# The order of the first transfers in a four-stage network: rows, weights, rows, tables, zeros

## The chip, the core and the metric

The kernel runs on one core of a Trainium2 chip. The core has five engines with queues of their own: PE (TensorE, matrix products), DVE (VectorE), ACT (ScalarE), POOL (GpSimd) and SP (SyncE), which here only starts transfers between the DRAM and the on-chip memory. The transfers are carried out by 16 DMA engines. PEld stands for TensorE's loads of weights, and a q after an engine's name for its sequencer.

The metric is the device time of one execution in microseconds (us), the median of several. L130 means line 130 of the kernel.

## What is computed

The input is X, 8 sequences of 512 rows of 256 values in float32. Four blocks follow, each with a normalised input, a normalised output and a residual sum:

```python
x = L0_attn_X
x = x + _layernorm(_L0_attn_ref(_layernorm(x), Wq, Wk, Wv, Wo, lq1, lk1, lq2, lk2, rms_scale))
x = x + _layernorm(_L0_ffn_ref(_layernorm(x), wqkv, q_scale, k_scale, wo, ln_g, ln_b, w1, b1, w2, b2))
x = x + _layernorm(_L1_attn_ref(_layernorm(x), Wqk_t, Wv_t, Wo_t, tau_t, ...))
x = x + _layernorm(_L1_ffn_ref(_layernorm(x), gate_w, w1, b1, ln1_g, ln1_b, w2, b2, ln_g, ln_b))
```

The first block is a causal attention with 16 heads in which two softmaxes are subtracted:

```python
Q, K, V = (proj(Wq), proj(Wk), proj(Wv))
lam = exp(sum(lq1 * lk1)) - exp(sum(lq2 * lk2)) + LAMBDA_INIT
attn = softmax(A1) - lam * softmax(A2)          # A1, A2: causal scores of the two halves
O = attn @ V
O = O / sqrt(mean(O * O) + EPS) * rms_scale * (1.0 - LAMBDA_INIT)
return Oc @ Wo.T
```

The second is a local attention of two layers (windows of 128 rows, 8 heads) with a gated feed-forward part; its queries and keys are normalised, scaled by q_scale and k_scale and rotated by a table of sines and cosines. The third is an attention by distances between rows. The fourth sends each row to 2 of 8 experts, by a table of rows in DRAM.

## The kernel before

**Stages.** The function network (L1230) calls four stages one after the other, each over all 8 sequences: diff (first block), local, diffusion and experts. A sequence is 4 tiles of 128 rows. All of X stays on chip in one tile, self.x, from which xb(b) takes the 4 row tiles of sequence b.

**What is loaded first.** begin (L119) loads the constants (L123), sets a small tile of -0.5 on GpSimd and loads the eight sequences of X, 512 KB each (L130). Then network calls, in this order:

- load_diff (L206): the first stage's weights wv, wq, wk and wo, 512 KB each, in one loop (L214); the scale rms in four small pieces (L218); VectorE multiplies wo by it (L220); the vectors lq and lk of both softmaxes (L225, L226), their products and sums (L227, L229) on VectorE, their exponentials (L230) on ScalarE, and from these the factor nlam (L234 to L239).
- clear_rows (L981): a 512 KB tile of zeros, set by GpSimd (L985), is stored 136 times (L988) into four tables of rows in DRAM, xrows and yrows for each of two parts. The tables are used by the stage of the experts only.
- load_projections (L453) for layer 0 of the local stage: the weight qkv, 1536 KB (L457), the rotary table rot, 512 KB (L459), and for q_scale and k_scale each three small pieces of a tile s (L462, L464). GpSimd multiplies the four parts of rot by s (L467). These tiles are in a pool named early. The local stage calls the function again for layer 1 (L531).
- diff (L258): the first stage itself.

**The first stage.** For a sequence, rows(b) normalises X (L155 and L157 on VectorE, L146 and L147 on GpSimd, L161 on VectorE, into h). prepare(b) turns h by transposes on TensorE (L172), copies the result to hT (L139 on ScalarE, L141 on VectorE), and makes v with wv (L180, L289). queries and keys make qT (L299) and kT (L310) with wq and wk for four heads at a time. A loop then runs over slots, eight to a step, eight steps to a sequence. In a slot, TensorE makes scores (sc, L322, and turned, sa, L332), VectorE adds the mask and takes maxima (L335, L336), ScalarE takes exponentials (e, L339), and GpSimd clears what lies above the diagonal (L342). Each step also has products with v (po, L355), sums of e by GpSimd (L360), and a division (pn, L373; L375 and L376 on ScalarE). The line of all matmuls that go through the helper mm is L180.

**What sets the order.** The text gives the operations and their dependencies. A planner fills each engine's queue before the kernel runs, from a model of the costs: an operation that stands early in the text can go to a later place in its engine's queue if the planner expects its input late. In the run, each queue is worked off in that fixed order, and semaphores hold an instruction until its inputs are there. All transfers of the opening are started by SyncE; its queue waits, too, when an earlier transfer has to be complete before another one starts.

Of the kernel before, what the change touches and what calls it, by code (L numbers as in the profile page):

```python
# [17 lines left out]
NB = 8  # L18
NT = 4
# [93 lines left out]
class Net:  # L113
# [5 lines left out]
    def begin(self, ctx):  # L119
        nc = self.nc  # L120
        keep = ctx.enter_context(self.tc.tile_pool(name="keep", bufs=1))
        self.const = keep.tile([P, C_N], F32, name="const", tag="const")
        nc.sync.dma_start(self.const, self.a["const"])  # L123
        self.ident = self.const[:, C_ID:C_ID + P]
        self.mhalf = keep.tile([P, 64], F32, name="mhalf", tag="mhalf")
        nc.gpsimd.memset(self.mhalf, -0.5)
        self.x = keep.tile([P, NB * NT, D], F32, name="x", tag="x")
        xin = self.a["L0_attn_X"].rearrange("b (t p) d -> p b t d", p=P)
        for b in range(NB):
            nc.sync.dma_start(self.x[:, b * NT:(b + 1) * NT, :], xin[:, b])  # L130

    def xb(self, b):
        return self.x[:, b * NT:(b + 1) * NT, :]
# [359 lines left out]
    def local(self, nb, early, first):  # L493
# [3 lines left out]
        with ExitStack() as ctx:  # L497
# [204 lines left out]
            for b in range(min(2, nb)):  # L702
                begin(b)
# [4 lines left out]
            for c in range(total + 1):  # L708
                if c + 1 < total:
                    r.add(rotated(c + 1))  # L710
                for u, calls in enumerate(slots):
                    if c < total:
                        scores(c, u)
                    if u == 2 and c:
                        g.add(gated(c - 1))
                    half = (len(calls) + 1) // 2
                    for f in calls[:half]:
                        f()
                    before = (c, u - 1) if u else (c - 1, 7)
                    if before in weights:  # L720
                        turned(*before)
                    for f in calls[half:]:
                        f()
                    if before[1] % 2 and (before[0], before[1] // 2) in sums:
                        attend(before[0], before[1] // 2)
                    if u in (2, 6) and c + 2 < nb:
                        save(c + 2) if u == 2 else begin(c + 2)
                qkv.pop(c - 1, None)
# [500 lines left out]
@with_exitstack  # L1229
def network(ctx: ExitStack, tc: tile.TileContext, a, out, nb=NB, parts=(1, 2, 3, 4)):  # L1230
    net = Net(tc, a, out)
    net.begin(ctx)
    if 4 in parts:
        net.scratch(ctx)
    with ExitStack() as local:
        early = local.enter_context(tc.tile_pool(name="early", bufs=1))
        with ExitStack() as w:
            if 1 in parts:
                net.load_diff(w)
            if 4 in parts:  # L1240
                net.clear_rows(w)
            if 2 in parts:
                first = net.load_projections(early, 0)
            if 1 in parts:
                net.diff(nb)
        if 2 in parts:
            net.local(nb, early, first)
    with ExitStack() as w:
        if 3 in parts:
            net.load_diffusion(w)  # L1250
            net.diffusion(nb)
    with ExitStack() as w:
        if 4 in parts:
            net.load_experts(w)
            net.experts(nb)
    if 4 not in parts:
        for b in range(nb):
            tc.nc.sync.dma_start(out.rearrange("b (t p) d -> p b t d", p=P)[:, b], net.xb(b))
# [39 lines left out]
```

## Time and profile before

| what | value |
|---|---|
| median of 3 runs | 4472.37 us (4471.97 to 4474.58) |
| the profiled execution | 4470.47 us |
| its span, first to last instruction | 4468.7 us |
| mean granted TensorE clock | 0.919 |
| bytes read from and written to HBM | 54.59 MB and 98.57 MB |
| stores of zeros (L988) | 136 of 512 KB, issued from 24.04 to 197.9 us |
| first and last mask of the first stage (L342) | 53.9 and 1167.1 us |
| first transposes of the local stage (L520) | 1196.9 us |
| first scatter of rows to the experts (L1094) | 3838.0 us |

How to read the lines that follow: the page gives each engine's busy time, its share of the span and its count of instructions; then the span in 40 equal slices of 112 us, where a digit is the busy share of a slice in tenths. A line of the table of waits has the waiting engine, line and operands, whom it waited for, and then the total, the number of times and the longest. A line of a timeline has the start, the duration, the engine, the line of code, the operation, output and inputs with their shapes, the count of merged instructions and, in brackets, how long the engine was idle before and what ended it. The lines of SPq are the transfers as SyncE starts them: their duration there is that of the start, not of the transfer.

### The profile page before, as it was taken

Reading aid. Unit: us, or ns where it says so; the run is one execution under the profiler, and the core shown is the slowest. Engines: PE = TensorE matmul, PEld = TensorE weight load, DVE = VectorE, ACT = ScalarE, POOL = GpSimd, SP = SyncE. Lnnn points to the kernel's source line nnn. Section 1 sums busy time; section 2 is a strip of 40 time slices with the busy share of each in tenths; the row PEclk is TensorE's granted clock in tenths of the full one; section 3 lists DMA queues with packets and bytes.
Section 4 is the critical chain, followed back from the end, with each engine's and each line's share of the span. In section 5 each row is a group of like instructions: output and inputs, shape, how many; then the busy total and the mean of one; then the engine's idle time right before and its main releaser. Section 6 shows DMA issues by size and latency. Waiting matters only on the chain.

```text
span 4468.7 us, 56341 instructions
## 1 busy us (share of the span) xinstructions
PE 3856.2 (86%) x21108; PEld 2000.8 (45%) x21108; DVE 2553.4 (57%) x4680; ACT 1760.7 (39%) x3300; POOL 1944.6 (44%) x1689
## 2 busy tenths in 40 slices
PE   8899999999778889999999998779999999488780
PEld 3333444433355555555555555433443434455450
DVE  6677777666365555444455554255666664454755
ACT  3455555555243333343433333224444443033230
POOL 3566666666565444444444454120111110441626
PEclk9999999999799999999999999889999999599895
DMA  9800000000000000000000000000000000421211
GB/s 382 347 6 1 6 6 6 6 6 6 30 3 3 3 3 3 3 22 9 27 8 8 8 8 10 13 19 1 1 1 1 1 1 1 156 76 59 79 55 61
DMA packets 101710, 160.97 MB, mean 36 GB/s; under 512 B 24956, under 2 KB 72384, under 8 KB 101440
## 3 DMA queue, kind: packets, MB, share of 16 engines
q1 hardware_dynamic: 95296, 140.59, 8.9%
q0 software_dynamic: 6144, 16.79, 1.2%
q8 instruction: 169, 2.77, 0.2%
q14 instruction: 101, 0.83, 0.1%
HBM read 54.59 MB, written 98.57 MB: 34 GB/s over the span
## 4 chain that ended last, share of the span: by engine, by line
PE 63%; POOL 16%; DVE 8%; SPq 4%; issue 4%; ACT 3%; DMA 1%; another core or an unknown queue 0%; POOLq 0%; DVEq 0%; ACTq 0%
PE lpa L180 8%; PE lpp L180 5%; PE tsc L832 5%; PE sc L322 5%; SPq L988 4%; PE pp L180 4%; PE po L355 3%; POOL ss L555 3%; PE py L180 3%; PE lqk L180 2%; PE tpo L855 2%; PE sa L332 2%; POOL qk L563 2%; PE ph L180 2%; PE lsc L597 2%
## 5 line engine op out<-in xcount | busy, mean ns | idle before, releaser
L339 ACT ACTIVATE e<-sa 128x1024 f32<-128x1024 f32 (+3 forms) x512 | 359.5, 702 | 355.1 <-PE sa L332 352.7
L360 POOL TENSOR_TENSOR e<-e,e 128x1536 f32<-128x1536 f32 (+2 forms) x192 | 451.6, 2352 | 93.6 <-PE po L355 83.7
L332 PE MATMUL sa<-qT,kT 32*128 32x512 f32 (+3 forms) x2048 | 432.6, 499 | 9.5 <-ACT e L339 9.1
L336 DVE TENSOR_REDUCE spread<-sc 128x2 f32<-128x256 f32 (+3 forms) x512 | 422.5, 825 | 15.6
L322 PE MATMUL sc<-kT,qT 32*128 32x128 f32 (+3 forms) x2048 | 422.7, 495 | 6.3 <-ACT kT L310 3.1
L844 DVE TENSOR_REDUCE spread<-tsc 128x2 f32<-128x1024 f32 x256 | 311.5, 1221 | 191.7 <-PE tsa L841 162.7
L847 ACT ACTIVATE te<-tsa 128x1024 f32<-128x1024 f32 x256 | 261.6, 1024 | 379.7 <-PE tsa L841 379.1
L180 PE MATMUL lpa<-ghT,lw 128*128 128x512 f32 (+1 forms) x768 | 378.2, 651 | 13.9 <-ACT ghT L525 13.9
L611 ACT ACTIVATE lp<-lp,lnm 128x256 f32<-128x256 f32 (+1 forms) x512 | 239.8, 470 | 217.5 <-DVE lnm L603 121.5
L335 DVE TENSOR_TENSOR sc<-sc,const 128x256 f32<-128x256 f32 x512 | 218.9, 428 | 181.5 <-PE sa L332 156.0
L146 POOL TENSOR_SCALAR rs<-mv 128x1 f32<-128x1 f32 (+1 forms) x208 | 41.5, 199 | 625.3 <-DVE mv L157 607.7
L841 PE MATMUL tsa<-tqT,tkT 32*128 32x512 f32 x1024 | 293.1, 652 | 22.9 <-DVE spread L844 22.7
L832 PE MATMUL tsc<-tkT,tqT 32*128 32x512 f32 x1024 | 302.5, 643 | 1.2 <-DVE tkT L818 0.7
L322 PEld LDWEIGHTS sc<-kT,qT 32*128 32x128 f32 x2048 | 159.9, 189 | 281.7 <-issue 123.0
L619 POOL TENSOR_TENSOR lp<-lp,lrs 128x256 f32<-128x256 f32 (+1 forms) x128 | 103.2, 828 | 395.7 <-DVE lrs L612 395.7
L615 POOL TENSOR_TENSOR lp<-lp,lrs 128x1024 f32<-128x1024 f32 x64 | 121.6, 1900 | 312.2 <-DVE lrs L612 302.3
L180 PEld LDWEIGHTS lpa<-ghT,lw 128*128 128x128 f32 (+1 forms) x768 | 147.1, 197 | 229.6 <-issue 197.6
L180 PE MATMUL lqk<-qkv,lhT 128*128 128x512 f32 x512 | 240.8, 613 | 1.4 <-ACT lhT L139 0.8
L342 POOL TENSOR_SCALAR_AFFINE_SELECT e<-e 128x512 f32<-128x512 f32 x256 | 160.5, 640 | 186.2 <-ACT e L339 186.1
L1168 ACT ACTIVATE ehT<-eht,enorm 128x128 f32<-128x128 f32 x320 | 120.2, 457 | 289.6 <-PE eht L1164 255.6
L555 POOL TENSOR_TENSOR ss<-ss,mhalf 128x16 f32<-128x16 f32 x64 | 186.2, 2909 | 82.5 <-DVE ss L554 81.7
L355 PE MATMUL po<-e,v 128*32 128x512 f32 (+3 forms) x2048 | 190.1, 454 | 19.4 <-POOL e L342 19.0
(256 smaller groups left out, 7743.7 us busy)
## 6 DMA issues: line engine op xcount, KB each, us to landing
xrows<-zero SPq DMA_DIRECT2D x68, 512.0 KB
yrows<-zero SPq DMA_DIRECT2D x68, 512.0 KB
ex<-xrows SPq DMA_DIRECT2D x80, 128.0 KB
yrows<-ey SPq DMA_DIRECT2D x80, 128.0 KB
ew<-in_L_ffn_w_dram SPq DMA_DIRECT2D x16, 512.0 KB
x<-in_L_attn_X_dram SPq DMA_DIRECT2D x8, 512.0 KB
saved<-x SPq DMA_DIRECT2D x8, 512.0 KB
lx<-saved SPq DMA_DIRECT2D x8, 512.0 KB
```

The lines of the kernel that those rows point to most:

```text
L180: self.nc.tensor.matmul(out, lhsT=l, rhs=r, start=i == 0, stop=i == len(pairs) - 1)
L322: nc.tensor.matmul(sc[:, i, :w], lhsT=qT[g, self.tok(t)], rhs=kT[g, :w], start=True, stop=True)
L332: nc.tensor.matmul(sa[:, i, :S - k * P], lhsT=kT[g, self.tok(k)], rhs=qT[g, k * P:], start=True, stop=True)
L336: nc.vector.tensor_reduce(self.spread[n % 2][:, t, g0:g0 + 2, 0 if n % 2 else 16], sc[:, :, :w], AX.X, ALU.max, negate=True)
L339: nc.scalar.activation(x[:, h0:h0 + 2, :], sa[:, :, :S - k * P], AF.Exp, scale=0.25)
L355: nc.tensor.matmul(pos[n][group(g), k * P:], lhsT=seqs[b][1][:, k, 4 * r + g, :], rhs=x[:, g, :], start=k == 0, stop=k == 2)
L360: nc.gpsimd.tensor_add(y, y, es.pop((n, k)))
L555: nc.gpsimd.tensor_tensor(sf, sf, self.mhalf[:, :2 * FH], ALU.pow)
L832: nc.tensor.matmul(sc[:, i, :], lhsT=qT[q, self.tok(t)], rhs=kT[q, :], start=True, stop=True)
L841: nc.tensor.matmul(sa[:, i, :], lhsT=kT[q, self.tok(k)], rhs=qT[q, :], start=True, stop=True)
L844: nc.vector.tensor_reduce(self.spread[n % 2][:, t, g0:g0 + 2, 16], sc, AX.X, ALU.max, negate=True)
L847: nc.scalar.activation(es[n, k][:, h0:h0 + 2, :], sa, AF.Exp)
```

## The change

The loop over the eight transfers of X becomes a function of its own. begin calls it for sequence 0 only. network calls it for sequences 1 to 7 after load_diff, then load_projections, and only then clear_rows.

```diff
@@ begin
         self.x = keep.tile([P, NB * NT, D], F32, name="x", tag="x")
+        self.load_rows(range(1))
+
+    def load_rows(self, seqs):
         xin = self.a["L0_attn_X"].rearrange("b (t p) d -> p b t d", p=P)
-        for b in range(NB):
-            nc.sync.dma_start(self.x[:, b * NT:(b + 1) * NT, :], xin[:, b])
+        for b in seqs:
+            self.nc.sync.dma_start(self.xb(b), xin[:, b])
@@ network
             if 1 in parts:
                 net.load_diff(w)
+            net.load_rows(range(1, NB))
+            if 2 in parts:
+                first = net.load_projections(early, 0)
             if 4 in parts:
                 net.clear_rows(w)
-            if 2 in parts:
-                first = net.load_projections(early, 0)
             if 1 in parts:
                 net.diff(nb)
```

In the order of the text, SyncE's transfers are then: const, x of sequence 0, wv, wq, wk, wo, rms, lq and lk, x of sequences 1 to 7, qkv, rot, s, and the 136 stores of zeros. No transfer, no operation and no byte is added or left out.

## The prediction

> **What bounds the kernel now.** I read the page first (busy shares and the 40 slices), then the table of waits of the first 300 us, then the timelines of SyncE, GpSimd, ScalarE and TensorE around the two places that the change touches. The page gives TensorE as the engine that sets the pace, and one odd stretch at the start: the DMA engines are full for the first two slices and idle after.
>
> ```profile
> PE 3856.2 (86%) x21108; PEld 2000.8 (45%) x21108; DVE 2553.4 (57%) x4680; ACT 1760.7 (39%) x3300; POOL 1944.6 (44%) x1689
> ...
> PE   8899999999778889999999998779999999488780
> ...
> DMA  9800000000000000000000000000000000421211
> ```
>
> The reader is to see that TensorE is at 8 tenths exactly in the slices in which the DMA engines are full (slices are 112 us). The table of waits for 188 to 232 us (engine and line, whom it waited for, total us, times, longest) says who lost time there:
>
> ```profile
> ACT e L339 <- PE sa L332: 24.3, 9, 18.2
> POOL rot L467 <- DMA s<-in_L_ffn_q_scale_dram: 22.0, 1, 22.0
> DVE sc L335 <- PE sa L332: 21.3, 5, 16.9
> PEld po L355 <- POOL e L342: 18.3, 3, 15.2
> PE po L355 <- POOL e L342: 15.4, 2, 14.3
> ```
>
> So it is a chain: GpSimd waits for a transfer, TensorE for GpSimd, ScalarE and VectorE for TensorE. The timeline of GpSimd shows where it stands (start, duration, line, operation, count, idle before):
>
> ```profile
> 187.12 0.63 POOL L342 TENSOR_SCALAR_AFFINE_SELECT e<-e 128x512 f32<-128x512 f32 x1
> 209.78 1.41 POOL L467 TENSOR_TENSOR rot<-rot,s 128x256 f32<-128x256 f32 x2 [22.03 <-DMA s<-in_L_ffn_q_scale_dram]
> 211.14 0.64 POOL L342 TENSOR_SCALAR_AFFINE_SELECT e<-e 128x512 f32<-128x512 f32 x1
> 211.75 1.41 POOL L467 TENSOR_TENSOR rot<-rot,s 128x256 f32<-128x256 f32 x2
> ```
>
> The multiplication of the rotary table, which only the local stage needs (its first matmuls come at 1197 us), stands in GpSimd's queue among the masks of the first stage, and nothing behind it can run. SyncE's timeline says why its operand is late: 136 stores of zeros are ahead of it.
>
> ```profile
> 24.04 41.73 SPq L988 DMA_DIRECT2D xrows<-zero  x34
> ...
> 154.18 43.72 SPq L988 DMA_DIRECT2D yrows<-zero  x34
> 197.94 2.09 SPq L457 DMA_DIRECT2D qkv<-in_L_ffn_wqkv_dram  x1
> 200.07 1.12 SPq L459 DMA_DIRECT2D rot<-in_rotary_dram  x1
> 201.24 1.00 SPq L462 DMA_DIRECT2D s<-in_L_ffn_q_scale_dram  x1
> ```
>
> The second place is the start. TensorE's timeline has its first projection waiting for the first weight, which SyncE issued behind all eight x transfers:
>
> ```profile
> 10.73 2.19 PE L172 MATMUL pt<-const,h 128*128 128x128 f32 x8 [10.73 <-DVE h L161]
> 18.80 1.19 PE L180 MATMUL pv<-wv,hT 128*128 128x512 f32 x1 [5.87 <-DMA wv<-in_wvT_dram]
> ```
>
> **What the Trainium skill says.** "TensorE: Matmul & The Clock Gate", section "Architectural detail: the array is 16× 32×32, not 1× 128×128": GpSimd's queue is a strict FIFO; the trace agrees (one waiting multiplication held masks whose inputs were made at about 189 to 198 us until 211.14). "DMA: Bandwidth & Descriptors", section "Queues, rings and completion order": on each DMA engine descriptors are consumed in the order of the ring, so a small transfer queues behind all bytes issued before it; the trace agrees (the 32 KB of s were in use only at 209.78, behind 136 stores). The first page's section "Part 1: The HAM clock gate (the "warmup" mystery)" has the array at half clock until it has been busy for some 3.4 us; here the first pv weight loads are 0.86 us apart until 24.05 and 0.43 after, so about six matmuls were slow, near 2.6 us in all.
>
> **The change, part by part.** The sum is made against the profiled execution: span 4468.7, device time 4470.5, so 1.8 us lie around the span; the median of the runs shown is 4472.4, 1.9 above that execution.
>
> Bytes and instructions are the same; only SyncE's order changes. Does that queue follow the text? In the trace it does at the start: const, eight x, wv, wq, wk, wo, rms, lq, lk, zeros, qkv, rot, s. GpSimd's doesn't: L467 stands far behind the first norm, which is later in the text; a planner set it by its own estimate of when s lands, and that was 22.0 us short.
>
> (1) *rot and s ahead of the zeros.* Ahead of s will be const 771.5 KB, x 8 x 512, weights 4 x 512, lq and lk 4 x 128, qkv 1536 and rot 512: 9475 KB or 9.70 MB. In before 301 GB/s x 25.0 us = 7.5 MB had moved at 25 us (windows view, first stretch); the other 2.2 MB at the 406 GB/s of the next stretches take 5.4, so 30.4. The six s transfers take 3.9 us to issue (201.24 to 205.16) and the last was in use 4.6 us later: s is there at about 39 us at worst. GpSimd has nothing to do from 19.5 (end of the last L147) to 53.93 (first mask): wherever the planner puts the four multiplications (0.73 us each, 2.9 in all) in that gap, their wait is covered by 14 us of slack; were they put behind the first masks, they would cost up to 2.9 and no wait.
>
> What the stall costs is read from the pace, not from the 22.0, since TensorE still had work. Line L375 (a reciprocal on ScalarE) runs once per step, eight steps to a sequence. Every eighth start, from ScalarE's timeline: 177.77, 331.93, 468.68, 604.84, 741.45, 878.06, 1014.12. The distances are 154.2, then 136.8, 136.2, 136.6, 136.6, 136.1. The stretch with the stall is 154.2 - 136.5 = 17.7 us longer than the others. This includes the slow clock after it (0.82 for 211.9 to 232). What is next late without it? In the same steps of other sequences nothing stands in for it: these distances are alike to 0.7 us, and TensorE is busy for 97.0 of 100 us at 300 to 400. So 17.7; the lower end 14.8 if the multiplications return to the path.
>
> (2) *First weights ahead of seven x transfers.* 512 KB at 406 GB/s is 1.29 us; seven are 9.0. wv, in use at 18.8, is then there at about 9.8; wq and wk follow at 1.29 each. The next late thing is hT: its second half is copied by VectorE at 12.96 for 0.69, so pv starts at 13.65: 5.15 earlier. Below this it is not certain: VectorE is in order too, and wo's scaling (L220, which waited for rms until 24.41; 9.0 earlier is 15.4) and the lq products (24.41 to 27.66 with waits, 3.3 us) may be planned ahead of that copy. Then hT would be at 15.4 + 3.3 + 0.7 = 19.4, 0.6 later than pv now: a loss of 0.6. Above it: without the pause from 12.92 to 18.80 the array may be warm sooner, up to 2.6 more, 7.8 in all. I take 4.5, since the copy of hT has the higher claim on being early (its inputs exist at 12.9, before rms can land), less a little for the mix. After pv the path is pv, pq, pk, kT, first scores at 33.12; all of it moves along.
>
> (3) *Seven x transfers later.* x1 follows lq and lk at about 15, x7 at about 15 + 6 x 1.29 + latency, 24 to 25. Needed early: nothing. TensorE turns the second sequence at 220.89; VectorE makes all 32 statistics before 22.0 only because it was idle. Moved, they fill VectorE's gaps; from 33.1 to 50.0 it was busy 11.65 of 16.9. If planned before x lands, a statistic holds VectorE by the planner's error, which was 22.0 in 210 us, so about 2 to 3 us at 25, before the first scores at 28.6. Cost 0, upper end 3.
>
> (4) *Zeros later.* They start about 2.1 MB of qkv and rot (5 us) and the issues of s later and end near 205 to 210, as the last transfer did. Their first user (L1094, the scatter of rows) runs at 3838 us. The next thing in SyncE's queue, L510 at 317.45, waited for GpSimd's x (103.0 us), not for the DMA. The s loads of layer 1 were hoisted by the planner to 211.22 and wait for L467; they may now hold the zeros up for some us. Free.
>
> Sum: 17.7 + 4.5 = 22.2. Profile: 4470.5 - 22.2 = 4448.3; beside the median: 4472.4 - 22.2 = 4450.2.
>
> **The rivals.** A, both gains: 4450; own range 4447 (17.7 + 7.8) to 4456 (14.8 + 1.5).
> B, the stall goes but the start gains nothing, because VectorE waits for rms or a late x ahead of hT or the first scores: 17.7, or 14.8 - 0.6 at worst: 4454 to 4458, middle 4455. For: the planner is optimistic about transfers. Against: these waits need a low-ranked operation ahead of a high-ranked one.
> C, the change doesn't remove the stall: something else on GpSimd or SyncE takes its place (the hoisted layer-1 loads, a norm of a late x), only the start gains: 4472.4 - 4.5 = 4468. Against: no wait in before has that operand, and slack is 14 us.
> D, slower: the planner, starting from other arrival times, lays out GpSimd's and TensorE's queues of the first stage's 64 steps otherwise. Its place is the step: L375 shows steps of 14.1 to 20.5 us by their contents; if one 14.1 step per sequence became a 20.4 one, 8 x 6.3 = 50 us come on top: 4500. It decides from 3.9 us per sequence on (31 us eat 22 and the 9 that can be measured). For: GpSimd's order in before is the planner's, and TensorE waits for GpSimd's L342 and L360 at every step. Against: after the 17.7 us disturbance the pattern of steps returns to the same values within 0.1 us, so the order is stable.
>
> **How the numbers follow.** A 0.62, B 0.18, C 0.07, D 0.13. About 0.2% (8.9 us) can be told from no change: faster is below 4463.4, slower above 4481.3. A and B are faster, 0.80; C is within, 0.07; D slower, 0.13. The range 4444 to 4468 holds A, B and about C, 0.8 to 0.87; its lower end leaves 3 us for what I have not counted.
>
> **What would show it.** L467 stands before 55 us and its wait blocks nobody; no entry "POOL rot" is behind a mask near 190; pv starts near 14 with hT, not wv, as its releaser; the first scores at about 28.6; the start of the eighth L375 at about 173, and all seven distances near 136.5. It is wrong if a distance over 140 stays (C or D), if pv still starts after 18 (B), or if the later stages, which the diff doesn't name, grow by more than 5 us.

## The result and the profile after

| | before | after |
|---|---|---|
| median of 6 runs each | 4472.44 us | 4452.55 us |
| ratio after/before, 95% interval | | 0.9956 (0.9943 to 0.9968) |
| the profiled execution, its span | 4470.47, 4468.7 us | 4452.14, 4450.4 us |
| first matmul with wv (pv) | 18.80 us | 12.65 us |
| first scores (sc) | 33.12 us | 25.01 us |
| first turned scores (sa) | 49.41 us | 44.13 us |
| start of the eighth step (L375, now L378) | 177.77 us | 174.57 us |
| from the eighth to the sixteenth step | 154.2 us | 137.0 us |
| first load for the local stage (lwo) | 1189.88 us | 1169.21 us |
| last copy of an expert tile's input (exT) | 4356.8 us | 4336.4 us |

The forecast was 4450.2, a gain of 22.2 us. The medians are 19.9 us apart, the two profiled executions 18.3.

Two words of the table need care. L375 (L378 after) takes the logarithm, Ln, by which the division is done; the prediction calls it a reciprocal. The step at 177.77 us is the seventh start of this line, not the eighth: the first is at 82.83. The prediction and the expectations call it the eighth and the one eight steps on the sixteenth, and these names are kept here. The distances don't depend on it: counted from the next start, 194.14, the one in before is 154.2 as well.

The lead is 3.2 us at the eighth step, 20.3 at the sixteenth, and stays between 20 and 21 through the local stage, the diffusion and the experts (last row: 20.4); only the last 100 us, gathers and norms on GpSimd and VectorE, gave 2 us back in this execution. So the change of time comes from the first 230 us. Lines of the kernel after stand 3 or 4 higher than before.

The page of after, busy shares and the rows of TensorE and of the DMA engines over 40 slices:

```profile
PE 3850.8 (87%) x21108; PEld 2000.2 (45%) x21108; DVE 2544.6 (57%) x4680; ACT 1760.6 (40%) x3300; POOL 1947.7 (44%) x1689
...
PE   8999999999688999999999998879999998488780
...
DMA  9900000000000000000000000000000000522211
```

The second slice of TensorE is now 9 with the DMA engines as full as they were. So the prediction's remark that TensorE is at 8 tenths exactly where the DMA engines are full named a coincidence; the row of before has 7 and 8 in later slices as well, with the DMA engines at 0. Where the table of waits had GpSimd's 22.0 us, the same stretch of after (185 to 229 us) is led by short repeated waits, none over 3.2 us:

```profile
ACT e L342 <- PE sa L335: 10.7, 13, 1.2
POOL e L345 <- ACT e L342: 9.6, 4, 3.2
DVE sc L338 <- PE sa L335: 6.2, 5, 1.5
```

GpSimd's timeline shows the multiplication in its new place, with 2.1 us of waiting for s in a stretch in which the engine had nothing else to do; the first mask comes 12.9 us after its end:

```profile
32.95 2.78 POOL L470 TENSOR_TENSOR rot<-rot,s 128x256 f32<-128x256 f32 x4 [2.08 <-DMA s<-in_L_ffn_q_scale_dram]
...
48.66 0.65 POOL L345 TENSOR_SCALAR_AFFINE_SELECT e<-e 128x512 f32<-128x512 f32 x1 [12.93 <-ACT e L342]
```

SyncE's timeline follows the text, and the stores of zeros end at 205 us:

```profile
20.31 1.42 SPq L460 DMA_DIRECT2D qkv<-in_L_ffn_wqkv_dram  x1
21.77 0.71 SPq L462 DMA_DIRECT2D rot<-in_rotary_dram  x1
22.52 0.43 SPq L465 DMA_DIRECT2D s<-in_L_ffn_q_scale_dram  x1
...
31.41 42.31 SPq L991 DMA_DIRECT2D xrows<-zero  x34
...
160.91 44.33 SPq L991 DMA_DIRECT2D yrows<-zero  x34
```

TensorE's timeline of the opening, the line of before for its second scores, and below them VectorE's timeline of after at the first scores:

```profile
10.42 2.19 PE L175 MATMUL pt<-const,h 128*128 128x128 f32 x8 [10.42 <-DVE h L164]
12.65 8.06 PE L183 MATMUL pv<-wv,hT 128*128 128x512 f32 x16
...
25.01 0.50 PE L325 MATMUL sc<-kT,qT 32*128 32x128 f32 x8 [0.87 <-ACT kT L313]
28.37 2.41 PE L325 MATMUL sc<-kT,qT 32*128 32x512 f32 x8 [2.86 <-DVE spread L339]
```

```profile
35.02 2.41 PE L322 MATMUL sc<-kT,qT 32*128 32x512 f32 x8 [1.40 <-DVE spread L336]
```

```profile
24.95 1.37 DVE L158 BATCH_NORM_STATS2 st<-x 128x6 f32<-128x256 f32 x4
26.24 0.36 DVE L160 BATCH_NORM_AGGREGATE mv<-st 128x2 f32<-128x6 f32 x4
26.52 0.72 DVE L158 BATCH_NORM_STATS2 st<-x 128x6 f32<-128x256 f32 x2
27.15 0.75 DVE L338 TENSOR_TENSOR sc<-sc,const 128x256 f32<-128x256 f32 x2
```

pv follows the transposes at once, with no wait for wv, and its 16 matmuls take 8.06 us where they took 10.02. But the first scores, there at about 25.5, are taken up by VectorE only at 27.15, since statistics of later sequences stand ahead of them; TensorE waits 2.86 us for the first maxima where it waited 1.40 in before (first scores at 33.12, the next at 35.02).

### The profile page after: what moved, and what is told of

It reads as the page before. It is cut to its first block, busy times and chain, and to the rows that moved or that the text cites. A ratio compares the mean times of both kernels' runs of the same rounds, so it can differ in the third digit from the quotient of the medians.

```text
span 4450.4 us, 56345 instructions
## 1 busy us (share of the span) xinstructions
PE 3850.8 (87%) x21108; PEld 2000.2 (45%) x21108; DVE 2544.6 (57%) x4680; ACT 1760.6 (40%) x3300; POOL 1947.7 (44%) x1689
## 4 chain that ended last, share of the span: by engine, by line
PE 66%; POOL 17%; DVE 9%; issue 4%; ACT 3%; DMA 1%; SPq 0%; POOLq 0%; DVEq 0%; ACTq 0%
PE lpa L183 8%; PE sc L325 6%; PE lpp L183 5%; PE tsc L835 5%; PE pp L183 4%; PE po L358 3%; PE sa L335 3%; POOL ss L558 3%; PE py L183 3%; PE lqk L183 2%; PE tpo L858 2%; POOL qk L566 2%; PE ph L183 2%; POOL rs L150 2%; PE lsc L600 2%
## 5 line engine op out<-in xcount | busy, mean ns | idle before, releaser
L339 DVE TENSOR_REDUCE spread<-sc 128x2 f32<-128x256 f32 (+3 forms) x512 | 422.2, 825 | 15.4
L684 DVE SCALAR_TENSOR_TENSOR u<-lpa,lb,gl 128x512 f32<-128x512 f32 x96 | 71.9, 749 | 233.0 <-ACT gl L683 233.0
```

Source lines behind the costliest of these rows:

```text
L339: nc.vector.tensor_reduce(self.spread[n % 2][:, t, g0:g0 + 2, 0 if n % 2 else 16], sc[:, :, :w], AX.X, ALU.max, negate=True)
```

## The experiments

Two theories of the gain. Mine: two separate gains, a freed GpSimd queue (17 us) and an earlier start (some 3 us). The rival: one effect, of the rows and weights or of the zeros' traffic. Two theories of the start, whose lead falls from 8.1 us (first scores) to 3.2 (eighth step): the statistics on VectorE, or TensorE's half clock. Experiments of one group ran beside their own runs of before, whose median was 4467.4 in the first group, 4468.4 in the second and 4465.7 in the third; every ratio is against these.

**One half of the change: tables_first.** Before, with load_projections ahead of clear_rows:

```diff
+            if 2 in parts:
+                first = net.load_projections(early, 0)
             if 4 in parts:
                 net.clear_rows(w)
-            if 2 in parts:
-                first = net.load_projections(early, 0)
```

> The eight x transfers stay ahead of the weights as in before; only qkv, rot and s go ahead of the zeros. Theory (two separate gains: a GpSimd queue freed, 17 us, and an earlier start, 3 us): 4472.4 - 17.5 = 4455; eighth step (the Ln of the division, L375) at 177.8 us as in before, the distance to the sixteenth 136.8 instead of 154.2. Rival (the gain comes from the weights and rows, not from the tables): 4469 or more, distance near 154. Rival (the planner's new layout, not the wait): distances of later sequences change by over 1 us.

Measured: 4449.2, ratio 0.9965 (0.9953 to 0.9977); first scores at 33.19, eighth step at 177.02, then 137.1. The start is that of before, the stall is gone, and the other distances are those of before within 0.5 us. This half alone is 18.2 us below its before; the whole change is 19.9, 19.3 and 16.2 below in its three groups.

**The other half: rows_late.** After, with clear_rows ahead of load_projections again.

> Rows 1 to 7 go behind the weights as in after; qkv, rot and s stay behind the zeros. Theory: only the start gains, 4472.4 - 3.2 = 4469; eighth step at 174.6 us, the distance to the sixteenth still about 154 with a wait of GpSimd for s of about 22 us. Rival (rows and weights are the gain): 4455.

Measured: 4465.6, ratio 0.9994 (0.9984 to 1.0004), no clear change. First scores at 24.61. The stall is back, in GpSimd's timeline:

```profile
190.18 1.23 POOL L345 TENSOR_SCALAR_AFFINE_SELECT e<-e 128x512 f32<-128x512 f32 x2
209.26 0.72 POOL L470 TENSOR_TENSOR rot<-rot,s 128x256 f32<-128x256 f32 x1 [17.86 <-DMA s<-in_L_ffn_q_scale_dram]
```

The eighth step came at 180.83, later than in before, against my expectation: its three steps from 131.91 on took 48.9 us instead of 45.4, with TensorE's granted clock at 0.67, 0.98 and 0.83 in the three stretches of 10 us from 140 to 170 (1.00 in after). The distance to the sixteenth was 150.1: by being later, GpSimd waited 17.9 instead of 22.0.

**The queue or the transfer: multiply_late.** All transfers as in before; the multiplication is traced at the head of the local stage and tied behind GpSimd's last addition of the first stage:

```diff
-                    nc.gpsimd.tensor_add(xs, xs, z)
+                    self.mark = nc.gpsimd.tensor_add(xs, xs, z).ins
...
+            with tc.issue_after(self.mark):
+                for k in range(2):
+                    self.scale_table(first, k)
```

> All transfers in the order of before; only the four multiplications of rot are tied behind GpSimd's last addition of the first stage. Theory (what costs is the place in GpSimd's queue, not the late transfer): distance from the eighth to the sixteenth step 136.8, no wait for s; the four multiplications (2.9 us) now stand at the border to the local stage, so 4455 to 4458. Rival (the 71 MB of zeros hold up something else in the first stage): 4470 or more, distance near 154.

Measured: 4450.6, ratio 0.9966 (0.9952 to 0.9980), distance 136.6. GpSimd's timeline has it at the border of the stages, after no wait:

```profile
1178.07 0.72 POOL L411 TENSOR_TENSOR x<-x,z 128x256 f32<-128x256 f32 x1 [0.66 <-DMA lw<-in_L_ffn_w_dram]
1178.75 2.77 POOL L473 TENSOR_TENSOR rot<-rot,s 128x256 f32<-128x256 f32 x4
```

The rot transfer was as late as ever (issued at 199.0). So what cost 17 us was the place in GpSimd's queue of an operation that nobody needed yet, not the late transfer and not the zeros' traffic.

**Doses: tables_half and tables_three_quarters.** After, with load_projections called from clear_rows behind two or three of its four tables.

> As after, but qkv, rot and s stand behind 68 of the 136 stores of zeros. Theory (the planner takes transfers as some 10 % faster than they are, so its error grows with the bytes ahead: 22.0 us behind 136 stores, 2.1 behind none): a wait of 11 to 12 us at about 125 us, of which some 4 are covered as in before, so 7 us on the path and 4452.5 + 7 = 4460. Rival (a fixed error of the planner): a wait of 2 us and 4452 to 4454, or of 22 us and 4469.

Measured: 4448.7, ratio 0.9960 (0.9946 to 0.9974); the multiplications at 122.3 to 125.0 with no wait for s at all. The six transfers of s were started by 114.9 us, before GpSimd came to the multiplication. The guess that the planner's error grows in proportion to the bytes ahead was wrong.

> As after, but qkv, rot and s stand behind 102 of the 136 stores. Behind 68 there was no wait, behind 136 one of 22.0 us. Theory (each further store costs 1.29 us on the chip against 0.96 in the plan): a wait of 8 to 9 us for s near 155 us, of which 4 to 5 are covered, so 3 to 5 us on the path against after. Rival (the wait at the full number has a cause of its own): no wait, and the time of after.

Measured: 4452.1, ratio 0.9960 (0.9946 to 0.9975), 3.0 us above after in the same group, which is within their spread. GpSimd's timeline:

```profile
155.76 0.64 POOL L345 TENSOR_SCALAR_AFFINE_SELECT e<-e 128x512 f32<-128x512 f32 x1
165.09 1.20 POOL L470 TENSOR_TENSOR rot<-rot,s 128x256 f32<-128x256 f32 x1 [8.69 <-DMA s<-in_L_ffn_q_scale_dram]
```

The wait and its price are those that were expected. The step with the stall took 18.5 us instead of 14.1, 4.4 more. With this the price of a wait can be read from three sizes: 8.7 us waited cost 4.4, 17.9 cost 13.3 (150.1 - 136.8), 22.0 cost 17.1 (154.2 - 137.0). Each time 4.3 to 4.9 us were covered by work that the other engines still had. The place that the planner gave moved 65.5 us (122.3 to 187.75) for 68 stores that took 88 us on the chip (SyncE: 110.06 to 197.94 in before), which suggests that the plan counts the stores as faster than they are; it wasn't tried by itself, and why the first 68 leave no wait isn't settled.

**Repeats of the changed kernel: after_again and after_third.**

> The changed kernel once more, beside the others on the same chip. Theory (the start gains some 3.5 us, with the half-clock stretches of TensorE moving it by up to 3 from one execution to the next): first Ln of the division between 77 and 83 us (79.7 in the first profile), distance from the eighth to the sixteenth step 137, time 18 to 20 below before. Rival (the start is the same in each execution): first Ln at 79.7 within 0.3.

> The changed kernel again, as the measure for the two beside it: 18 to 20 us below before, first scores at 25 to 26, first turned scores (sa) near 44.5, first Ln between 77 and 83, distance from the eighth to the sixteenth step 137.

Measured: 4449.1, ratio 0.9958 (0.9941 to 0.9974), and 4449.5, ratio 0.9960 (0.9945 to 0.9975). The distances are 137.0 and 136.6. The first Ln came at 78.32 and 82.11 (79.66 in the first profile), in the same program. The windows view says what differed; the columns are the stretch, its length, busy us and counts of the engines, then the granted clock, DMA share and GB/s. First after, then after_third:

```profile
45.00:55.00 10.00, 9.29 (x37) 5.03 (x36) 6.92 (x10) 3.67 (x4) 1.28 (x2) 0.68 1.02 404
55.00:65.00 10.00, 9.93 (x40) 4.07 (x41) 4.72 (x9) 2.61 (x5) 1.27 (x2) 0.50 1.02 406
65.00:75.00 10.00, 10.00 (x82) 4.19 (x76) 7.53 (x13) 4.96 (x8) 8.37 (x5) 0.96 1.02 404
```

```profile
45.00:55.00 10.00, 10.00 (x32) 4.20 (x28) 6.28 (x9) 3.12 (x4) 0.65 (x1) 0.50 1.02 402
55.00:65.00 10.00, 9.92 (x44) 5.52 (x42) 4.34 (x9) 2.51 (x5) 1.91 (x3) 0.50 1.02 406
65.00:75.00 10.00, 10.00 (x76) 3.60 (x70) 6.58 (x9) 4.63 (x6) 6.66 (x3) 0.80 1.03 407
```

Summing length times (1 - clock) in stretches of 5 us from 20 to 85 us gives the TensorE time lost to the clock: 10.3 us in after_again, 13.6 in after, 17.1 in after_third, with the first Ln at 78.3, 79.7 and 82.1. One program varies by 3.8 us at the first Ln, and the lost time with it; that is as much as the gain that is looked for there.

**The statistics: rows_after_zeros, const_second, const_second_only, statistics_tied.** First, the seven later x behind 34 of the stores (called from clear_rows behind its first table), and the same with x of sequence 0 ahead of the constants:

> As after, but x of the sequences 1 to 7 is loaded behind 34 of the stores of zeros, so that the statistics of these rows are out of VectorE's queue while the first scores are made. Theory (these statistics hold the first maxima up and cost 2.8 us of the start's lead): the first scores again at 25.0, the first turned scores (sa) at 41 to 42 instead of 44.1, first Ln at 76 to 79. Rival (the half clock alone eats the lead): sa at 44 as in after. Risk: a late x holds VectorE up near 75 us, then the eighth step comes later than 174.6.

> As rows_after_zeros, and x of sequence 0 ahead of the 771 KB of constants. Theory (the norm waits only for x): the first statistics at about 5.0 instead of 6.85 us, first scores at about 23.3 to 24, so 1 to 2 us below rows_after_zeros. Rival (the transposes wait for the identity in the constants, which land as before): first scores at 25.0, no gain.

Measured: 4460.1, ratio 0.9982 (0.9973 to 0.9990), and 4458.1, ratio 0.9978 (0.9968 to 0.9987): both behind after. The first part of the theory held: sc at 25.96 and sa at 40.51 in rows_after_zeros, 14.6 us between them instead of 19.1, and 24.19 and 38.74 in const_second, 1.8 us earlier still. The rest did not. VectorE's timeline of rows_after_zeros at 79 us:

```profile
78.86 0.41 DVE L338 TENSOR_TENSOR sc<-sc,const 128x256 f32<-128x256 f32 x1
80.37 1.38 DVE L164 TENSOR_SCALAR h<-x,mv,rs 128x256 f32<-128x256 f32 x4 [1.10 <-POOL rs L150]
81.67 0.95 DVE L339 TENSOR_REDUCE spread<-sc 128x2 f32<-128x768 f32 x1
```

The norms now stand among the maxima of a busy stretch: VectorE waits for GpSimd's rs in the middle of a slot, between a mask and its maximum. With the 28 statistics of seven sequences between 77 and 98 us, the first Ln came as late as 89.9 and the eighth step at 183.98. I had feared that a late x would hold VectorE; none did (its one wait for x, 6.7 us, is that for the first). The work itself was in the way.

> As after, only x of sequence 0 goes ahead of the constants. Theory (the norm waits for x alone, seen as 1.8 us in const_second): first scores at 23.2 to 24.2; the lead ends in the same place as after's, since VectorE is held by the statistics, so 0 to 2 us below after. Rival (all of it stays): 2 us or more below after.

```diff
-        nc.sync.dma_start(self.const, self.a["const"])
...
         self.load_rows(range(1))
+        nc.sync.dma_start(self.const, self.a["const"])
```

Measured: 4448.5, ratio 0.9960 (0.9946 to 0.9974), beside 4449.5 of after_third: no difference that these runs can tell. Scores at 23.73 instead of 24.93, and TensorE then waits 4.65 us for the first maxima.

> As const_second_only, and the norm of each later sequence is tied on VectorE behind the maximum of the slot at which the text has it, so that its statistics leave the opening but don't come in a bunch. Theory (the statistics hold up the first maxima; spread out they cost nothing): first turned scores at 39 us, first Ln at 74 to 77, eighth step at 168 to 171, 3 to 5 us below after. Rival (the lead is eaten by the half clock whatever VectorE does): first Ln at 78 to 80, the time of after. Rival (the tie costs in the other sequences): distances over 138.

```diff
-                    rows(n // 8 + 1)
+                    with self.tc.issue_after(self.top):
+                        rows(n // 8 + 1)
```

(self.top is the last maximum traced on VectorE.) Measured: 4504.0, ratio 1.0077 (1.0064 to 1.0091), slower than before. The distances are 146.9 and then five times 146.8, against some 136.5: 10 us for each sequence. In its timelines of GpSimd, VectorE and TensorE, in this order:

```profile
202.66 2.35 POOL L363 TENSOR_TENSOR e<-e,e 128x1024 f32<-128x1024 f32 x1
204.95 0.64 POOL L345 TENSOR_SCALAR_AFFINE_SELECT e<-e 128x512 f32<-128x512 f32 x1
205.68 0.19 POOL L149 TENSOR_SCALAR rs<-mv 128x4 f32<-128x4 f32 x1
205.95 1.01 POOL L150 TENSOR_TENSOR rs<-rs,mhalf 128x4 f32<-128x4 f32 x1
```

```profile
207.00 2.63 DVE L164 TENSOR_SCALAR h<-x,mv,rs 128x256 f32<-128x256 f32 x4 [4.31 <-POOL rs L150]
```

```profile
207.77 0.47 PE L175 MATMUL pt<-const,h 128*128 128x128 f32 x1 [5.05 <-DVE h L164]
```

The statistics were done at 202.36, but GpSimd was in its sums of e, so its part of the norm began 3.3 us later; VectorE waited 4.31 us for it with maxima behind, and TensorE 5.05 and then 0.79 for h. These waits account for 5.8 of the 10 us; where the rest goes isn't shown. This is what the forecast's case D describes, an order of the queues that costs in every sequence, brought about here by one misplaced norm per sequence. And the first Ln came at 84.13 with 18.8 us lost to the clock, although sa was at 41.32. So the statistics do delay sa: without them it follows sc by 1.6 us (statistics_tied) to 4.8 us (const_second) sooner than in const_second_only. But that lead didn't reach the first Ln in either run, nor in rows_after_zeros.

The starts side by side (us; 8 to 16 is the distance between these steps, lost is the time lost to the clock up to 85 us):

| kernel | sc | sa | first Ln | eighth | 8 to 16 | lost |
|---|---|---|---|---|---|---|
| before | 33.12 | 49.41 | 82.83 | 177.77 | 154.2 | 10.2 |
| tables_first | 33.19 | 49.43 | 82.16 | 177.02 | 137.1 | 8.5 |
| multiply_late | 32.80 | 51.57 | 85.81 | 180.74 | 136.6 | 15.4 |
| after | 25.01 | 44.13 | 79.66 | 174.57 | 137.0 | 13.6 |
| after_again | 26.04 | 44.97 | 78.32 | 173.26 | 137.0 | 10.3 |
| after_third | 24.93 | 44.52 | 82.11 | 181.34 | 136.6 | 17.1 |
| rows_late | 24.61 | 44.05 | 81.64 | 180.83 | 150.1 | 17.1 |
| tables_half | 24.96 | 44.30 | 79.10 | 175.54 | 139.0 | 13.6 |
| tables_three_quarters | 26.06 | 44.99 | 83.62 | 181.32 | 136.7 | 18.8 |

The eighth step of tables_three_quarters lies behind its stall, and the 139.0 of tables_half holds a dip of the clock (0.83 from 190 to 200 us).

The last column says more than the three repeats do. Within each of the two orders the first Ln comes later by about 0.6 us for each us lost, and at equal loss it comes about 5 us sooner in the new order: before has 82.83 with 10.2 lost, after_again 78.32 with 10.3. (A line with this slope and this step, fitted to all nine rows, misses none by more than 0.8 us.) So the lead at sa, 5.3 us in after, may well be kept, and hidden by a larger loss: the new order lost 15.1 us on average, the old one 11.4. This is arithmetic on nine profiles, not an experiment, and whether the new order brings the larger loss about isn't shown. The granted clock doesn't count everything either: in before it reads 1.00 from 20 to 25 us, where the loads of pv are 0.86 us apart until 24.05.

No version was found that beats the changed kernel by more than the runs can tell.

## Why the prediction was right

- *Which engine waits for what.* Right. tables_first and multiply_late remove the stall in two ways that share nothing but GpSimd's queue, and rows_late brings it back. The order of bytes in the rings, which the prediction names for the lateness of s, can only be a part of it: GpSimd was free for the multiplication from 187.75 us on, and SyncE started the first transfer of s at 201.24, so 13.5 of the 22.0 us passed before that transfer was started at all, while SyncE was still starting the last stores, qkv and rot.
- *Size of the stall,* 17.7 from the pace: measured 17.1 by the same distance (154.2 - 137.0; 17.1 to 17.6 with the other runs that have no stall and no dip there). Taking the price from the distance between steps and not from the 22.0 us of the wait was what made it right: the cover of 4.3 to 4.9 us shows in all three sizes of the wait.
- *The slack for the new place.* The table was ready at 32.95, before my bound of 39, and the first mask came at 48.66. The 2.9 us of multiplication cost nothing there.
- *The start,* 4.5, with -0.6 and 7.8 as ends: 3.2 at the eighth step in the profile of after. That the two are near each other is luck, since the steps inside were mis-sized and the errors offset each other. pv began at 12.65, not 13.65: its first matmuls waited for ScalarE's half of hT only, not for VectorE's. And the array was at full pace sooner, the prediction's upper end (loads of pv 0.43 us apart from 14.96 on; 8.06 us for pv instead of 10.02). So the first scores came 8.1 us earlier, beyond that upper end. Neither wo's scaling nor the lq products stood ahead of hT. Then the lead shrank, by 2.8 us up to sa and by 2.1 more up to the first Ln. "All of it moves along" was the step of this part that failed.
- *The late x,* "cost 0, upper end 3": the cost was not 0. The planner put statistics ahead of the first masks (24.95 to 27.15), and TensorE's wait grew from 1.40 to 2.86 us. rows_after_zeros shows that without them sa comes 4.5 us sooner after sc.
- *What the start is worth in the end* stays open within some 3 us: the first Ln has a mean of 83.6 us in the three profiles with the order of before and 80.7 in the six with the new one, and repeats of one program lie 3.8 apart. In the whole time it isn't seen: rows_late alone has a ratio of 0.9994 (0.9984 to 1.0004), and tables_first, without the new start, is as far below before as the whole change is.
- *How much the sum proves.* In the profiled execution the forecast of 22.2 is 3.9 too high: 0.6 in the stall, 1.3 in the start, and 2.0 that the last 100 us gave back. The stated range, 4444 to 4468, would also have held a start that gains nothing, so that the time fell into it bears out the stall, not the start.
- *Zeros later, layer-1 loads.* Free, as forecast; the hoisted loads of s for layer 1 were put behind the zeros (205.34 us), not ahead of them.
- *Case D* didn't occur here: the later distances are 136.8, 136.3, 136.1, 136.6 and 136.2. statistics_tied shows that it is real.

## What to carry to other kernels

An operation that prepares data for a later stage can stop the present one if it stands in an in-order queue and its operand comes late: look for a long wait of an engine that isn't the busiest, and ask whether what stands behind it needs that operand. Free it by bringing the operand forward or by moving the operation back; both gave the same here. Price such a stall by the pace of the loop across it, not by the length of the wait. And before moving light work out of an idle opening, see where it lands: the statistics that VectorE made in an idle opening, up to 22 us in before, cost 10 us or more where they stood among the maxima.

## What was unexpected of the hardware

TensorE was at half clock for long stretches in which its matmuls followed each other without a gap: 45 to 65 us in after_third, 9.92 and 10.00 us busy of 10, granted clock 0.50. (The ends of matmuls are modelled in the profile, so short pauses may be hidden.) Busy us are stretched by the slow clock, yet this is several times the 3.4 us of activity after which the Trainium skill ("TensorE: Matmul & The Clock Gate", section "Part 1: The HAM clock gate (the "warmup" mystery)") has the array back at full speed. Dips of a few us came later too, in some executions of the same program and not in others (0.70 from 140 to 150 us in after_third, 1.00 in after). In the six profiles of the table with the new order, the time lost up to 85 us and the start of the first Ln rise together, from 10.3 and 78.3 us in after_again to 18.8 and 83.6 in tables_three_quarters. What brings the half clock about isn't shown.
